# Sums written over gathered rows, and 41 held parts of the table instead of 40

## The chip, the cores and the metric

The kernel runs on one core of one Trainium2 chip. The metric is the device time of one execution in microseconds (us); lower is better. The engines are named as the profile names them: PE (matrix multiply; its weight loads are PEld), DVE (vector), ACT (scalar), POOL (GpSimd, here the issuer of gathers) and SP (SyncE, the issuer of most transfers; SPq and ACTq are the issuing queues of SP and ACT).

## The reference, cut to what matters

```python
e = emb[seq]                                   # 1024 users, 50 steps, 128 numbers
prefix = jnp.cumsum(e, axis=1)
uF = prefix / jnp.minimum(t + 1, lengths)      # per step and user
y = (uF - mean_over_users) * rsqrt(var + 1e-5) * gamma + beta
# 50 steps, one after the other:
v = v + (x - v) / 2; spike = (v >= 1); v = v - spike
scores = spikes.mean(over steps) @ emb.T       # 1024 x 100001, float32
```

Row 0 of the table counts as zero. The output has 409.6 MB, the table 51.2 MB.

## The kernel before, in words

**Two stages.** The first runs the 50 steps (`for t in range(T)`, line 384). The second multiplies the spike counts (eight blocks of 128 users, `counts[0..7]`) with the transposed table, evicts, scales and stores. PE works in a format of about half the float32 digits, so each part of the table is *split* into a high and a low half and multiplied twice (`product`, lines 198 to 207).

**A step.** `gather(t)` (line 245) lets POOL issue eight indirect transfers of 128 rows each into a tile `e`; the pool `gather` has two such tiles, which alternate. In five steps (`BY_SYNC`: 12, 22, 31, 40, 49) it issues seven, and SP fetches the last 128 rows one by one (`fetch_singles`, line 261). PE transposes the rows onto running sums in PSUM (`pre`, line 391). DVE scales the sums into a tile `uF` of a pool of its own (line 402) and takes the statistics (403, 414). ACT takes the square root (418) and turns `uF` into mean minus `uF`, in place (425). DVE works out the factor `a` (431 to 444), ACT forms the scaled x in `vt` out of `uF` (line 448), and DVE adds the decayed old state (451). The gathers of step t+2 stand in the program right behind the statistics of step t (line 404), so they need the tile `e` of step t, which is free when PE has read it. POOL has nothing else to do in the steps.

**Parts.** The table has 98 parts of 1024 rows (the last has 673). A part is loaded as a tile of 128 partitions by 1024 numbers (4 KB in each partition). 40 are *held*: loaded while the steps run, 14 of them at the start, two more into places of parts 0 and 1, which are split in the steps 42 and 44 (lines 470 to 482), and 24 (groups 2 to 5 of six parts) when SP has issued its last single rows (line 409). The other 58 are loaded in the second stage, three at a time, by ACT's queue (`fetch`, line 141), into row tiles whose parts have been split.

`pick` (line 130) loads one part in three in another way: its rows on partitions 0 to 119 by an indirect transfer from POOL, the other eight partitions by ACT or by a second indirect transfer, with small dummy transfers (`turn_by`) between them. `PICKED` lists these parts.

**Splitting.** `prepare` (line 189) lets PE transpose a part (line 177), ACT copy the high half (193) and DVE subtract it for the low half (194). A pair of places for the halves must be free (`free`). At first there are two pairs and `third` (the tile `aside`, which held parts 2 and 3). When all six parts of a row tile have been split, its space becomes three pairs (`places`, line 546): after part 9 and after part 15.

**Products.** `WIDTHS` cuts the 98 parts into column blocks: four of two parts, four of three, thirteen of six. Column block 0 consists of parts 0 and 1, and so on. In each, the eight user blocks n follow one another; a part's product goes to one of four PSUM tiles and is evicted by ACT or DVE in turn (lines 605 and 607) into an output tile, and SP stores the whole output tile (`store`, line 209). Output tiles take turns (`turns`): four of two parts in column blocks 0 to 3, three of three parts in blocks 4 to 7, three of six parts from 8 on, of which two are row tiles. A tile is written again when its store has ended. `ready` (line 572) is called behind user blocks 2 to 6 and behind each part of block 7 (in column block 0 from 4, from 8 on from 0); it splits the next part if a pair is free and the part belongs to this column block, the next one, or one of the `FURTHER` ones. All engines work in program order.

Of the kernel before, what the change touches and what calls it, by code (L numbers as in the profile page):

```python
# [30 lines left out]
TWICE = 2  # L31
ASIDE = 2
SHIFT = TWICE + ASIDE
FURTHER = {5: 1, 6: 2}

# [4 lines left out]
SPARED = 120  # L40
PICKED = range(42, 97, 3)
TURN = 17
# [6 lines left out]
def rec_kernel(  # L49
# [46 lines left out]
    def pair(i):  # L96
        free.append([embp.tile([P, HALF], F32R, tag=f"{x}{i}", name=f"{x}_{i}") for x in ("hi", "lo")])

    def size(q):
        return min(HALF, N - q * HALF)  # L100
# [4 lines left out]
    def group(g):  # L105
        at = g if g < AHEAD else AHEAD - 2 + g % 2
        r = rowp.tile([P, GROUP, HALF], F32, tag=f"rows{at}", name=f"rows_{g}")
        for k in range(GROUP):
            rows[g * GROUP + SHIFT + k if g else k + ASIDE * (k >= TWICE)] = r[:, k, :]
        return r  # L110
# [76 lines left out]


    def prepare(q, pt):
        turned(q, pt)  # L190
        split[q] = hi, lo = free.pop(0)
        vp, vh, vl = views(q, pt, hi, lo)
        nc.scalar.copy(vh, vp)  # L193
        nc.vector.tensor_tensor(vl, vp, vh.bitcast(F32), ALU.subtract)  # L194
# [18 lines left out]
    with ExitStack() as ph:  # L213
        once = ph.enter_context(tc.tile_pool(name="once", bufs=1))
        lp = ph.enter_context(tc.tile_pool(name="lif", bufs=1))
        sp = ph.enter_context(tc.tile_pool(name="stats", bufs=3))
        up = ph.enter_context(tc.tile_pool(name="uF", bufs=1))
        gp = ph.enter_context(tc.tile_pool(name="gather", bufs=2))
# [11 lines left out]
        nc.sync.dma_start(out=gb[:, 1:2], in_=beta.rearrange("(d o) -> d o", o=1))  # L230
        first = group(0)
        fetch(first, 0, 0, TWICE)
        spare = asidep.tile([P, ASIDE, HALF], F32, tag="aside", name="spare")
        for k in range(ASIDE):
            rows[TWICE + k] = spare[:, k, :]
        fetch(spare, 0, TWICE, ASIDE)
        fetch(first, TWICE, SHIFT, GROUP - TWICE)
        for g in range(1, EARLY):
            fetch(group(g), 0, g * GROUP + SHIFT, GROUP)
# [34 lines left out]
        make_identity(nc, ident)  # L274
        isz = up.tile([P, NB, P], F32, tag="uF", name="isz")
        rb = up.tile([P, NB, P], F32, tag="uF", name="rb")
        gather(0)
# [31 lines left out]
        for n in range(NB):  # L309
            nc.tensor.transpose(rps[:, n * P : (n + 1) * P], rb[:, n, :], ident)  # L310
        rlen = once.tile([P, B], F32, tag="rlen", name="rlen")
        nc.vector.tensor_copy(rlen, rps)
# [71 lines left out]
        for t in range(T):  # L384
            last = t == T - 1
            e = es.pop(t)
            uF = up.tile([P, B], F32, tag="uF", name=f"uF_{t}")
            bs = sp.tile([P, B // BANK, 6], F32, tag="bs", name=f"bs_{t}")
            for h, cs in enumerate(halves):
# [13 lines left out]
                nc.vector.bn_stats(bs[:, h, :], uF[:, cs])  # L403
            if t + 2 < T:
                gather(t + 2)
            if t in BY_SYNC[:-1]:
# [46 lines left out]
            if not last:  # L453
                vt = vp.tile([P, B], F32, tag=f"v{(t + 1) % 2}", name=f"v_{t}")
                x(vt, whole)
                if t:
                    spiked(count, whole, v)
# [40 lines left out]
        o0 = gp.tile([P, HALF], F32, tag="e", name="o_0_0")  # L498
        o1 = gp.tile([P, HALF], F32, tag="e", name="o_0_1")
        firsts = [(q, po, o, h, cs) for q, po, o in ((0, po0, o0), (1, po1, o1)) for h, cs in enumerate(halves)]  # L500
# [42 lines left out]
    to_fetch = held  # L543
    third = None

    def places(at):
        t = rowp.tile([P, GROUP, HALF], F32R, tag=f"rows{at}", name=f"pairs_{at}")
        free.extend((t[:, k, :], t[:, k + 1, :]) for k in range(0, GROUP, 2))

    for c, W in enumerate(WIDTHS):  # L550

        if c in (0, NARROW, MIDDLE):
            opening.close()
            if c == NARROW:
                assert third in free
                free.remove(third)
                beside.close()
            where = opening if c < MIDDLE else ctx
            op = where.enter_context(tc.tile_pool(name="o", bufs=1, reuse_waits="tile"))
            if c == 0:  # L560
                turns = [(op, f"o{k}", 2) for k in range(4)]
            elif c == NARROW:
                turns = [(op, f"o{k}", 3) for k in (2, 0, 1)]
            else:
                fourth = op.tile([P, 4, HALF], F32R, tag="pairs", name="pairs")
                free.extend((fourth[:, k, :], fourth[:, k + 1, :]) for k in (0, 2))
                turns = [(rowp, "rows2", 6), (op, "o", 6), (rowp, "rows3", 6)]
            blocks = 0
        q1 = q0 + W
        q2 = q1 + (WIDTHS[c + 1] if c + 1 < len(WIDTHS) else 0)  # L570

        def ready():
            nonlocal to_split, third
            if to_split < q2 + FURTHER.get(c, 0) and free:
                prepare(to_split, psum.tile([P, HALF], F32, tag="ps", name=f"pt_{to_split}"))
                to_split += 1

                if to_split == SHIFT:
                    t = asidep.tile([P, ASIDE, HALF], F32R, tag="aside", name="third")
                    third = (t[:, 0, :], t[:, 1, :])  # L580
                    free.append(third)
                if to_split in (GROUP + SHIFT, 2 * GROUP + SHIFT):
                    places(to_split // GROUP - 1)

# [65 lines left out]
```

## Time and profile before

| | before |
|---|---|
| median of 3 runs | 1556.75 us (1555.91 to 1557.61) |
| the profiled execution | 1554.93 us |
| its span on the core | 1552.9 us |
| PE, DVE, ACT, POOL busy in it | 1129.4, 950.0, 674.7, 431.1 us |
| HBM read, written | 77.69 MB, 409.60 MB |
| mean granted clock of PE | 0.961 |

The span is the time from the first to the last instruction of the core. The page gives busy time by engine, digits for 40 equal slices (tenths of a slice), the chain of work that ended last, and groups of instructions by source line. In a timeline row stand the start, the duration, the engine, the line, the operation, the tile written and the tiles read, and in brackets the idle time of the engine before it and what ended it; "issue" means that the profile shows nothing that was waited for. In a row of a table of stretches stand from and to, the length, the busy time of PE, PEld, DVE, ACT and POOL with the number of instructions, the granted clock of PE, the mean busy share of the 16 DMA engines and the GB/s that they moved.

### The profile page before, as it was taken

The page shows a single profiled execution, that of the slowest core. Times are in us where ns is not written, and L with a number is a line of the kernel's source. Part 1 is how long each engine was busy: PE and PEld are TensorE (multiplying, and loading weights), DVE is VectorE, ACT ScalarE, POOL GpSimd, SP SyncE. Part 2 cuts the span into 40 slices and gives each one's busy share as a digit, 9 for nine tenths or more (in the row PEclk, how much of TensorE's full clock was granted, in tenths as well). Part 3 has the DMA queues.
Part 4 walks back from the last instruction along what each step waited for, and adds up shares of the span by engine and source line. Part 5 has one row for each costly group of instructions (what it writes and reads, how often), then busy time and mean ns, then how long its engine had stood idle before and what let it go on. Part 6 is the DMA issues. An engine that isn't in the chain of part 4 may idle for free.

```text
span 1552.9 us, 13699 instructions
## 1 busy us (share of the span) xinstructions
PE 1129.4 (73%) x4465; PEld 799.3 (51%) x4465; DVE 950.0 (61%) x1128; ACT 674.7 (43%) x698; POOL 431.1 (28%) x462
## 2 busy tenths in 40 slices
PE   4444444454445998899988888887888888888894
PEld 2111111121222776677766666665666666666673
DVE  5777777677778656666555555554655555555552
ACT  3333333343334545555444444444444444444542
POOL 7777777777776000000010100101000010100000
PEclk9999999999999999999999998999989898999998
DMA  6222222832221999999999999999999999999999
GB/s 241 55 55 54 54 55 54 303 127 53 53 79 46 371 412 410 424 412 398 433 418 431 424 429 428 426 426 425 427 425 429 425 424 431 426 429 428 426 426 385
DMA packets 54315, 488.22 MB, mean 314 GB/s; under 512 B 12383, under 2 KB 13280, under 8 KB 33124
## 3 DMA queue, kind: packets, MB, share of 16 engines
q1 hardware_dynamic: 32176, 431.19, 66.0%
q0 software_dynamic: 16656, 35.60, 8.0%
q10 hardware_dynamic: 5412, 20.56, 3.2%
q8 instruction: 35, 0.57, 0.1%
q14 instruction: 36, 0.29, 0.1%
HBM read 77.69 MB, written 409.60 MB: 314 GB/s over the span
## 4 chain that ended last, share of the span: by engine, by line
DMA 42%; POOL 20%; PE 18%; issue 11%; DVE 5%; ACT 4%; ACTq 0%; SPq 0%; DVEq 0%; POOLq 0%
DMA scores<-o 40%; POOL e L248 20%; PE po L201 17%; DVE o L605 3%; ACT o L607 3%; DMA e<-in_L_rec_emb_table,idx 2%; DVE pairs L194 1%; ACT pairs L193 1%; PE pt L177 1%; ACT hi L193 0%; PE pre L391 0%; DVE lo L194 0%; PE warm L377 0%; DMA idx<-in_r_seq 0%; ACTq L607 0%
## 5 line engine op out<-in xcount | busy, mean ns | idle before, releaser
L605 DVE TENSOR_SCALAR o<-po 128x1024 f32<-128x1024 f32 (+1 forms) x390 | 467.6, 1215 | 307.6 <-PE po L201 154.3
L607 ACT ACTIVATE o<-po 128x1024 f32<-128x1024 f32 x392 | 393.4, 1025 | 487.7 <-DMA scores<-o 320.7
L248 POOL DMA_INDIRECT e<-in_L_rec_emb_table,idx x395 | 374.2, 947 | 122.4 <-issue 118.3
L391 PE MATMUL pre<-ident,e 128*128 128x128 f32 x395 | 174.7, 463 | 222.0 <-DMA e<-in_L_rec_emb_table,idx 221.7
L201 PE MATMUL po<-pairs,countB 128*128 128x512 f32 (+1 forms) x1120 | 287.8, 403 | 42.7 <-ACT o L607 42.7
L201 PE MATMUL po<-pairs,countC 128*128 128x512 f32 (+1 forms) x840 | 244.0, 438 | 61.2 <-ACT o L607 55.2
L201 PEld LDWEIGHTS po<-pairs,countB 128*128 128x128 f32 x1120 | 207.0, 189 | 104.4 <-ACT o L607 58.8
L391 PEld LDWEIGHTS pre<-ident,e 128*128 128x128 f32 x395 | 72.8, 185 | 327.0 <-DMA e<-in_L_rec_emb_table,idx 325.4
L201 PEld LDWEIGHTS po<-pairs,countC 128*128 128x128 f32 x840 | 170.1, 210 | 115.1 <-ACT o L607 65.4
L123 POOL DMA_INDIRECT rows<-in_L_rec_emb_table,picks x19 | 18.6, 980 | 636.3 <-PE pt L177 633.6
L194 DVE TENSOR_TENSOR pairs<-pt,pairs 128x1024 fp32r<-128x1024 f32 x70 | 85.3, 1218 | 101.5 <-ACT pairs L193 101.4
L402 DVE SCALAR_TENSOR_TENSOR uF<-rlen,pre 128x512 f32<-128x512 f32 x100 | 68.3, 683 | 101.9 <-PE pre L391 101.9
L177 PE MATMUL pt<-ident,rows 128*128 128x128 f32 (+1 forms) x768 | 106.0, 284 | 10.0 <-DVE rows L174 4.9
L177 PEld LDWEIGHTS pt<-ident,rows 128*128 128x128 f32 (+1 forms) x768 | 95.2, 148 | 27.2 <-issue 10.8
L418 ACT ACTIVATE r<-mv,eps 128x1 f32<-128x1 f32 x50 | 14.8, 295 | 213.8 <-DVE mv L414 213.8
L201 PE MATMUL po<-hi,countB 128*128 128x512 f32 x208 | 85.8, 412 | 12.5 <-ACT o L607 11.0
L349 PE MATMUL pre<-zT,ls 128*128 128x512 f32 x100 | 78.1, 783 | 22.5 <-DVE uF L402 18.5
L193 ACT CAST pairs<-pt 128x1024 fp32r<-128x1024 f32 x70 | 70.0, 1012 | 40.2 <-PE pt L177 40.2
L115 POOL DMA_INDIRECT turned_by<-in_L_rec_emb_table,picks x30 | 28.7, 956 | 209.8 <-DMA turned_by<-in_L_rec_emb_table,picks 198.7
L201 PE MATMUL po<-lo,countB 128*128 128x512 f32 x208 | 83.6, 402 | 0.0
L361 ACT ACTIVATE d<-v,less 128x1024 bf16<-128x1024 f32 x49 | 54.6, 1114 | 65.4 <-DVE v L451 62.3
L201 PE MATMUL po<-hi,countC 128*128 128x512 f32 x156 | 67.3, 432 | 13.8 <-ACT o L607 12.7
(99 smaller groups left out, 996.6 us busy)
## 6 DMA issues: line engine op xcount, KB each, us to landing
scores<-o SPq DMA_DIRECT2D x96, 3072.0 KB
scores<-o SPq DMA_DIRECT2D x32, 1536.0 KB
scores<-o SPq DMA_DIRECT2D x29, 1024.0 KB
scores<-o SPq DMA_DIRECT2D x8, 2896.5 KB
rows<-in_L_rec_emb_table ACTq DMA_DIRECT2D x19, 1024.0 KB
rows<-in_L_rec_emb_table SPq DMA_DIRECT2D x5, 3072.0 KB
held_rows<-in_L_rec_emb_table SPq DMA_DIRECT2D x640, 0.5 KB
e<-in_L_rec_emb_table,idx POOLq DMA_INDIRECT x395, 2.5
```

What stands on the lines that cost most here:

```text
L115: nc.gpsimd.indirect_dma_start(out=turned_by[:m, :], out_offset=None, in_=table.rearrange("n (k d) -> (n k) d", d=2), in_offset=bass.Indir ...
L177: nc.tensor.transpose(pt[:, k0 : k0 + pw], r[:pw, k0 : k0 + D], ident[:pw, :pw])
L193: nc.scalar.copy(vh, vp)
L194: nc.vector.tensor_tensor(vl, vp, vh.bitcast(F32), ALU.subtract)
L201: nc.tensor.matmul(po[:, :kw], lhsT=counts[n], rhs=part[:, k0 : k0 + kw], start=j == 0, stop=j == 1,)
L248: nc.gpsimd.indirect_dma_start(out=es[t][:, n * P : (n + 1) * P], out_offset=None, in_=table, in_offset=bass.IndirectOffsetOnAxis(ap=idx[: ...
L349: nc.tensor.matmul(pre[h], lhsT=l, rhs=zT[:, h * BANK : (h + 1) * BANK], start=t == 0, stop=False, skip_group_check=True,)
L361: nc.scalar.activation(d, v, AF.Identity, bias=less)
L391: nc.tensor.matmul(pre[h][:, k : k + P], lhsT=singles[t] if h * BANK + k + P == B and t in singles else e[:, h * BANK + k : h * BANK + k + P],
L402: nc.vector.scalar_tensor_tensor(uF[:, cs], rlen[:, cs], 1.0 / (t + 1), pre[h], ALU.max, ALU.mult)
L605: nc.vector.tensor_scalar_mul(o[:, h0 : h0 + hw], po[:, :hw], 1.0 / T)
L607: nc.scalar.mul(o[:, h0 : h0 + hw], po[:, :hw], 1.0 / T)
```

## The change

- The pool `uF` is gone: `uF = e`. DVE writes the scaled sums over the gathered rows of the step. `gather(t + 2)` moves down behind `x(vt, whole)`, so that it waits for line 448 of step t in place of the transposes.
- `isz` and `rb` of the preamble use the space of `negv`, and `rlen` becomes the second half of a new tile `shared`, whose first half holds part 4.
- 41 parts are held. Group 0 and 1 become six tiles of two parts (`two0` to `two10`), each loaded by a transfer of its own; `two0` is loaded twice, as before. The start loads 15 parts in eight transfers, where it were 14 in four.
- A tile of two parts becomes one pair of places when both have been split (`EMPTIED`: behind parts 6, 8, 10, 12, 14 and 16). `third` is free behind part 3 and is not used for parts from 8 on (`place_for`).
- In column blocks 0 and 1 there are three output tiles; from column block 2 on `shared` is the fourth.
- 57 parts are loaded in the second stage, 18 of them by `pick`, in 19 transfers of three; `FURTHER` lets column block 7 split one part more.
- One of the first outputs lies in `zT` in place of a gather tile.

```diff
-ASIDE = 2
+ASIDE = 3
 SHIFT = TWICE + ASIDE
-FURTHER = {5: 1, 6: 2}
+EMPTIED = {SHIFT + 2 + k: f"two{(k + 2) % GROUP if k < GROUP else k}" for k in range(0, 2 * GROUP, 2)}
+FURTHER = {5: 1, 6: 2, 7: 1}
...
-PICKED = range(42, 97, 3)
+PICKED = range(43, 95, 3)
...
+    def two(k, q):
+        r = rowp.tile([P, 2, HALF], F32, tag=f"two{k}", name=f"two_{q}")
+        rows[q], rows[q + 1] = r[:, 0, :], r[:, 1, :]
+        return r
...
+    def place_for(q):
+        return next((i for i, p in enumerate(free) if q < NARROW * WIDTHS[0] or p is not third), None)
...
-        split[q] = hi, lo = free.pop(0)
+        split[q] = hi, lo = free.pop(place_for(q))
...
-        up = ph.enter_context(tc.tile_pool(name="uF", bufs=1))
...
-        first = group(0)
+        first = two(0, 0)
         fetch(first, 0, 0, TWICE)
-        spare = asidep.tile([P, ASIDE, HALF], F32, tag="aside", name="spare")
-        for k in range(ASIDE):
+        spare = asidep.tile([P, ASIDE - 1, HALF], F32, tag="aside", name="spare")
+        shared = asidep.tile([P, 2, HALF], F32, tag="shared", name="shared")
+        for k in range(ASIDE - 1):
             rows[TWICE + k] = spare[:, k, :]
-        fetch(spare, 0, TWICE, ASIDE)
-        fetch(first, TWICE, SHIFT, GROUP - TWICE)
-        for g in range(1, EARLY):
+        rows[SHIFT - 1] = shared[:, 0, :]
+        rlen = shared[:, 1, :]
+        fetch(spare, 0, TWICE, ASIDE - 1)
+        fetch(shared, 0, SHIFT - 1, 1)
+        for k in range(2, 2 * GROUP, 2):
+            q = k + ASIDE + 2 * (k >= GROUP)
+            fetch(two(k, q), 0, q, 2)
+        for g in range(2, EARLY):
             fetch(group(g), 0, g * GROUP + SHIFT, GROUP)
...
-        isz = up.tile([P, NB, P], F32, tag="uF", name="isz")
-        rb = up.tile([P, NB, P], F32, tag="uF", name="rb")
+        isz = once.tile([P, NB, P], F32, tag="negv", name="isz")
+        rb = once.tile([P, NB, P], F32, tag="negv", name="rb")
...
-        rlen = once.tile([P, B], F32, tag="rlen", name="rlen")
...
-            uF = up.tile([P, B], F32, tag="uF", name=f"uF_{t}")
+            uF = e
...
-            if t + 2 < T:
-                gather(t + 2)
...
                 x(vt, whole)
+                if t + 2 < T:
+                    gather(t + 2)
...
-        o1 = gp.tile([P, HALF], F32, tag="e", name="o_0_1")
+        o1 = once.tile([P, HALF], F32, tag="zT", name="o_0_1")
...
-                turns = [(op, f"o{k}", 2) for k in range(4)]
+                turns = [(op, f"o{k}", 2) for k in range(3)]
...
+        elif c == 2:
+            assert to_split >= SHIFT
+            turns.append((asidep, "shared", 2))
...
-                if to_split == SHIFT:
-                    t = asidep.tile([P, ASIDE, HALF], F32R, tag="aside", name="third")
+                if to_split == SHIFT - 1:
+                    t = asidep.tile([P, ASIDE - 1, HALF], F32R, tag="aside", name="third")
                     third = (t[:, 0, :], t[:, 1, :])
                     free.append(third)
-                if to_split in (GROUP + SHIFT, 2 * GROUP + SHIFT):
-                    places(to_split // GROUP - 1)
+                if to_split in EMPTIED:
+                    t = rowp.tile([P, 2, HALF], F32R, tag=EMPTIED[to_split], name=f"pair_{to_split}")
+                    free.append((t[:, 0, :], t[:, 1, :]))
```

More of the change, by code (lines that the diff above doesn't have):

```diff
@@ L108, in group @@
         for k in range(GROUP):
-            rows[g * GROUP + SHIFT + k if g else k + ASIDE * (k >= TWICE)] = r[:, k, :]
+            rows[g * GROUP + SHIFT + k] = r[:, k, :]
         return r
@@ L185, in views @@
         )
+    third = None
+    def place_for(q):
+        return next((i for i, p in enumerate(free) if q < NARROW * WIDTHS[0] or p is not third), None)
     def prepare(q, pt):
         turned(q, pt)
-        split[q] = hi, lo = free.pop(0)
+        split[q] = hi, lo = free.pop(place_for(q))
         vp, vh, vl = views(q, pt, hi, lo)
@@ L543, in rec_kernel @@
     to_fetch = held
[L544 to L548, printed above, removed]
     for c, W in enumerate(WIDTHS):
@@ L554, in rec_kernel @@
             if c == NARROW:
-                assert third in free
-                free.remove(third)
+                assert any(p is third for p in free)
+                free[:] = [p for p in free if p is not third]
                 beside.close()
@@ L573, in ready @@
             nonlocal to_split, third
-            if to_split < q2 + FURTHER.get(c, 0) and free:
+            if to_split < q2 + FURTHER.get(c, 0) and place_for(to_split) is not None:
                 prepare(to_split, psum.tile([P, HALF], F32, tag="ps", name=f"pt_{to_split}"))
                 to_split += 1
-                if to_split == SHIFT:
-                    t = asidep.tile([P, ASIDE, HALF], F32R, tag="aside", name="third")
+                if to_split == SHIFT - 1:
+                    t = asidep.tile([P, ASIDE - 1, HALF], F32R, tag="aside", name="third")
                     third = (t[:, 0, :], t[:, 1, :])
                     free.append(third)
-                if to_split in (GROUP + SHIFT, 2 * GROUP + SHIFT):
-                    places(to_split // GROUP - 1)
+                if to_split in EMPTIED:
+                    t = rowp.tile([P, 2, HALF], F32R, tag=EMPTIED[to_split], name=f"pair_{to_split}")
+                    free.append((t[:, 0, :], t[:, 1, :]))
         blockwise = [(n, q) for n in range(1 if c == 0 else 0, NB) for q in range(q0, q1)]
```

## The prediction

> **What bounds the kernel now.** I read the page first, its slices above all, for they show two kernels in one.
>
> ```profile
> span 1552.9 us, 13699 instructions
> ...
> DMA  6222222832221999999999999999999999999999
> ...
> DMA 42%; POOL 20%; PE 18%; issue 11%; DVE 5%; ACT 4%; ACTq 0%; SPq 0%; DVEq 0%; POOLq 0%
> ```
>
> For the first third the DMA engines are mostly idle, apart from a load at the start and a burst in slices 8 and 9; these are the 50 steps. Then the DMA digits are all 9: the products, whose stores and loads fill the DMA engines. The chain agrees: POOL (GpSimd) and issue hold 31% of the span, DMA 42%. To see what kind of bound each is, I took the groups of lines (busy and mean ns, then idle time and what ended it) and the table of stretches (the last two columns are the DMA share and GB/s).
>
> ```profile
> L248 POOL DMA_INDIRECT e<-in_L_rec_emb_table,idx x395 | 374.2, 947 | 122.4 <-issue 118.3 <-DMA idx<-in_r_seq 2.3 <-PE pre L391 1.2
> 280.00:330.00 50.00, 23.45 (x51) 9.77 (x51) 35.56 (x61) 18.17 (x20) 37.80 (x41) 1.00 0.83 304
> 900.00:1000.00 100.00, 81.24 (x359) 63.13 (x358) 53.23 (x46) 44.07 (x45) 8.47 (x9) 0.94 1.01 427
> ```
>
> All 395 gathers go back to back: of 122.4 us idle, 118.3 is "issue" (0.30 each), and the 1.2 us put down to PE are four times that same 0.30. GpSimd never waits for a tile. So the steps last as long as GpSimd needs for its list of gathers, and **a microsecond that GpSimd is made to wait is never won back**. In the products the DMA share is 1.01 at 427 GB/s: there a byte less is time won, and a moment in which no store is queued is time lost.
>
> **The change, part by part.** The profiled run took 1554.93 us (span 1552.9); the median of the runs shown is 1556.75, 1.82 above it. I sum against 1554.93 and add 1.82 at the end. What a measurement of this kernel can tell from no change is about 0.2%, 3.1 us.
>
> *The step's tile is held longer.* Before, a gather tile is free once PE has transposed it; after, when ACT has read the scaled sums out of it (line 448), since they now lie in it. The gathers of step t+2 need that tile, so the question is whether line 448 of step t ends before GpSimd reaches them. Steps have eight gathers, five of them seven, so each can be counted off. The timeline gives start and duration.
>
> ```profile
> 3.33 0.19 DVE L280 CAST ids<-idx 128x50 f32<-128x50 int32 x1 [3.33 <-DMA idx<-in_r_seq]
> 3.59 1.14 POOL L248 DMA_INDIRECT e<-in_L_rec_emb_table,idx  x1 [2.27 <-DMA idx<-in_r_seq]
> 3.56 0.47 SPq L148 DMA_DIRECT2D spare<-in_L_rec_emb_table  x1
> ...
> 23.90 1.21 ACT L448 ACTIVATE v<-uF,hgb,a 128x1024 f32<-128x1024 f32 x1
> 24.64 0.94 POOL L248 DMA_INDIRECT e<-in_L_rec_emb_table,idx  x1 [0.30 <-PE pre L391]
> ...
> 208.66 1.21 ACT L448 ACTIVATE v<-uF,hgb,a 128x1024 f32<-128x1024 f32 x1 [0.64 <-DVE a L444]
> 213.15 0.94 POOL L248 DMA_INDIRECT e<-in_L_rec_emb_table,idx  x1 [0.31 <-issue]
> ...
> 301.19 1.21 ACT L448 ACTIVATE v<-uF,hgb,a 128x1024 f32<-128x1024 f32 x1 [0.64 <-DVE a L444]
> 301.81 0.94 POOL L248 DMA_INDIRECT e<-in_L_rec_emb_table,idx  x1 [0.30 <-PE pre L391]
> ...
> 320.31 1.21 ACT L448 ACTIVATE v<-uF,hgb,a 128x1024 f32<-128x1024 f32 x1 [0.63 <-DVE a L444]
> 320.53 0.94 POOL L248 DMA_INDIRECT e<-in_L_rec_emb_table,idx  x1 [0.30 <-PE pre L391]
> ```
>
> The first pair gives the price of a wait: the same transfer released DVE at 3.33 and GpSimd's gather at 3.59, so a gather starts about 0.3 us after its release. An ordinary step (19, with the gathers of 21) ends line 448 at 208.66 + 1.21 = 209.87, and the gathers start at 213.15: 3.28 us in hand, 3.0 after the 0.3. No cost there. Three steps have nothing in hand. Step 0 starts late and ends at 25.11, when gather 24.64 has gone out: a wait of 0.47 + 0.3 = 0.77. In the burst of 280 to 330 (304 GB/s: the loads of the groups 2 to 5) the gathered rows land later and the step ends later. Step 28 ends at 302.40 against 301.81: 0.59 + 0.3 = 0.89. Step 30 ends at 321.52 against 320.53: 0.99 + 0.3 = 1.29. Every wait moves the later gathers and their steps alike, so the waits add: **+2.95**. Behind the waiting gather stand only more gathers, and PE and DVE of that step wait for those. The lower bound is 0.77, if the burst falls so that the other two vanish (SyncE issues four more loads at the start, at 0.47 each by the row of `spare`, and so reaches it 1.9 us later); the upper is 3.5, for the start carries one part more and can make step 1 late too. I take the sum: GpSimd and burst shift by about the same amount.
>
> *One part less is loaded in the products.* 1024 x 512 bytes, 0.524 MB, at 427 GB/s: **-1.23**. Its load goes to the start instead. Bounds -1.23 and 0 (first rival).
>
> *Places for split parts come free two by two.* Before, the third pair and a group's three pairs were all there was, so part 7 was split at the last chance, part 9 with part 10 too. Following `ready` through both versions, part 7 is now split at block 3 of its predecessor, part 9 likewise, and only part 10 is left for the end of column block 3. Three dips of the DMA rate belong to these ends (the row of 706 is for a later part):
>
> ```profile
> 566.00:568.00 2.00, 2.00 (x6) 1.53 (x5) 1.59 (x2) 0.00 (x0) 0.00 (x0) 0.50 0.80 332
> 586.00:588.00 2.00, 1.66 (x5) 0.86 (x5) 2.00 (x2) 0.04 (x1) 0.00 (x0) 1.00 0.70 291
> 590.00:592.00 2.00, 2.00 (x10) 1.59 (x9) 1.23 (x1) 1.11 (x2) 0.00 (x0) 1.00 0.71 297
> 706.00:708.00 2.00, 2.00 (x10) 1.63 (x9) 2.00 (x3) 1.03 (x1) 0.00 (x0) 1.00 0.79 330
> ```
>
> Against 427 the first loses 2 x (1 - 332/427) = 0.44 us, the second 0.64, the third 0.61. The first and third go; the second stays, for a split still stands there: **-1.05**, bounds 0 and -1.69.
>
> *Three output tiles instead of four in column blocks 0 and 1.* The fourth is the tile with part 4, and comes in column block 2. What it costs shows best at the end of column block 1:
>
> ```profile
> 506.40 1.36 SPq L210 DMA_DIRECT2D scores<-o  x3
> 506.00:508.00 2.00, 1.77 (x7) 0.86 (x6) 1.89 (x4) 1.95 (x4) 0.00 (x0) 1.00 0.37 137
> ...
> 540.74 1.03 ACT L607 ACTIVATE o<-po 128x1024 f32<-128x1024 f32 x1 [1.60 <-DMA scores<-o]
> 542.70 1.23 DVE L194 TENSOR_TENSOR lo<-pt,hi 128x1024 fp32r<-128x1024 f32 x1 [3.35 <-ACT hi L193]
> 543.84 2.37 DVE L605 TENSOR_SCALAR o<-po 128x1024 f32<-128x1024 f32 x2
> 545.12 1.48 SPq L210 DMA_DIRECT2D scores<-o  x2
> ...
> 556.84 1.03 ACT L607 ACTIVATE o<-po 128x1024 f32<-128x1024 f32 x1 [1.56 <-DMA scores<-o]
> ...
> 562.05 1.03 ACT L607 ACTIVATE o<-po 128x1024 f32<-128x1024 f32 x1 [1.58 <-DMA scores<-o]
> ```
>
> Stores free a tile every 2.60 us (556.84 to 562.05 is two of them). Block 7 got its tile at 540.74; a split's cast and its subtraction (542.70) come behind it, and its store goes out at 545.12. With three tiles it waits for one store more: 543.34, and the store goes out at 547.7. At 540.74 three stores were still under way, which last to 540.74 + 3 x 2.60 = 548.5 as counted by the freeing of tiles. Bytes trail an issue by about a microsecond: the first stores are issued at 506.40, and 506 to 508 has 0.37 of its 2 us in use, so they start at 507.3. I estimate the same for a freeing behind the last byte. So the engines run out at 547.5 and start again at 548.7: 1.2 us. An ordinary block takes 1.2 us from tile to store, and with two stores of 2.60 queued nothing runs dry. **+1.2**, bounds 0 (the trailing times are shorter) and 3.0 (the same again where column block 0 opens and ends).
>
> *One more split at the end of column block 7* (the new entry of `FURTHER`), one less in block 8. There DVE is behind already:
>
> ```profile
> 705.52 1.22 DVE L194 TENSOR_TENSOR pairs<-pt,pairs 128x1024 fp32r<-128x1024 f32 x1
> 706.65 2.35 DVE L605 TENSOR_SCALAR o<-po 128x1024 f32<-128x1024 f32 x2
> ```
>
> The subtraction of 1.22 at 705.52 holds back the last eviction, and the DMA dip of 706 to 708 (0.79) is there. A second one puts another 1.2 in front of that store; the split that block 8 is spared gives part of it back, in dips that are as short. **+0.7**, bounds 0 and 1.2.
>
> *The rest at nothing:* `rlen` in half a tile, `isz` and `rb` under `negv`, the last load of three parts, the second first output in `zT`. All are ahead of or beside the waits above; uncovered, they cost a fraction of a step, inside the 3.5.
>
> Sum: 2.95 - 1.23 - 1.05 + 1.2 + 0.7 = +2.57; 1554.93 + 2.57 + 1.82 = **1559.3**.
>
> **The rivals.**
>
> *The DMA engine of the last eight partitions sets the pace.* `pick` spares the rows from 120 on in some loads: before in 19 of 58 loaded parts, after in 18 of 57, which leaves 39 unspared both times. If the engine that serves these rows bounds the products, the part less wins nothing: +3.80, 1560.6. Against it: a mean share of 1.01 over 16 engines leaves none of them idle to wait for a slower one. The profile shows no single engine, so it is not excluded. The Trainium skill (DMA: Bandwidth & Descriptors, section Latency and other measured facts) says that DMA engines 7 and 15 are usually slower than the others in traces; no run here shows it, and by that rule this rival would hold.
>
> *GpSimd's waits in the burst vanish.* If the burst starts 1.9 us later and GpSimd only 0.77, the steps 28 and 30 may end in time: 0.77 in place of 2.95, +0.39, 1557.1. With the bounds of the dips as well, a gain reaches -2.2. For it: the shortfalls, 0.59 and 0.99, are smaller than that shift. Against it: the burst lasts through four steps, and some step lies at its end wherever it starts.
>
> *Slower: three tiles starve the stores.* It decides when tile-to-store takes more than the 5.2 us of two queued stores less the two trailing microseconds, 3.2. Evictions in pairs take 1.2; with a split between, the rows above show 545.12 - 540.74 = 4.4. If PE, too, stands still while four PSUM tiles wait, ordinary blocks lose about 0.4 each: 12 x 0.4 = 4.8 in place of 1.2, +6.17, 1562.9. Against it: at column block 4 three tiles already serve, with bigger stores.
>
> **How the numbers follow.** My case 0.50, the vanished waits 0.25, the slow engine 0.13, the starved stores 0.12. My case reaches past +3.1 in three of ten, since its middle is at +2.57 and its terms are uncertain by about 1; the vanished waits stay within, and 0.06 of it is kept for a gain over 3.1, which lies outside every bound above; the slow engine is half and half. Slower: 0.15 + 0.12 + 0.07 = 0.34; faster 0.06; the same 0.60. The range takes in the vanished waits with the best dips (1556.75 - 2.2 = 1554.6) and the starved stores: 1554.6 to 1563.0.
>
> **What would show it.** Right: L248 shows idle time put down to ACT L448, about 3 us in three places (near 25, 302 and 322), and the last gather comes that much later; the dips at 566 and 590 are gone, new ones stand near 548 and 708; loads issued by ACT carry one part less. Wrong: waits of GpSimd in ordinary steps (then the tile is held longer than line 448, and every step would pay), no waits at all, or a DMA rate below 427 in the long middle.

## The result and the profile after

| | before | after |
|---|---|---|
| median (16 runs each, one chip) | 1556.26 us (1554.94 to 1558.40) | 1560.11 us (1559.12 to 1561.12) |
| ratio, 95% interval | | 1.0025 (1.0018 to 1.0032) |
| profiled execution, its span | 1554.93, 1552.9 us | 1560.22, 1558.4 us |
| first store issued | 506.40 us | 509.27 us |
| first store to the end of the span | 1046.5 us | 1049.1 us |

The change costs 3.85 us, 0.25%. The forecast was 1559.3 us, +2.57. The last two rows say where it went: 2.87 us into the steps, 2.6 us into the products. That makes 5.5 for two single executions, which overstates it: before's profiled one lay 1.3 below its median. In the experiments, three executions on one chip were in a slower state, at 2020, 1942 and 1672 us, and are left out of the medians.

The page of the changed kernel looks like the page of before; the chain has moved its shares from POOL and issue to DMA, though the steps are as long as ever. So it is no measure of what bounds them.

```profile
span 1558.4 us, 14089 instructions
...
DMA  7222222832121899999999999999999999999998
...
DMA 50%; PE 19%; POOL 13%; issue 6%; DVE 6%; ACT 4%; ACTq 0%; SPq 0%; DVEq 0%; POOLq 0%
```

The waits of the changed kernel up to the end of the steps (total, times, longest) have a line that before did not have, and the timeline has the places.

```profile
POOL e L264 <- issue: 106.4, 349, 0.3
...
POOL e L264 <- ACT v L461: 4.0, 4, 1.5
```

```profile
25.45 0.94 POOL L264 DMA_INDIRECT e<-in_L_rec_emb_table,idx  x1 [1.17 <-ACT v L461]
...
291.85 1.21 ACT L461 ACTIVATE v<-e,hgb,a 128x1024 f32<-128x1024 f32 x1 [0.50 <-DVE a L457]
293.33 0.94 POOL L264 DMA_INDIRECT e<-in_L_rec_emb_table,idx  x1 [1.00 <-ACT v L461]
...
323.24 0.94 POOL L264 DMA_INDIRECT e<-in_L_rec_emb_table,idx  x1 [1.52 <-ACT v L461]
...
499.71 0.94 POOL L264 DMA_INDIRECT e<-in_L_rec_emb_table,idx  x1 [0.30 <-issue]
```

Of four waits for line 461 one is the usual 0.30; the others exceed it by 0.87, 0.70 and 1.22. The pair at 291.85 shows the mechanism: line 461 ends at 293.06 and the gather starts 0.27 later. The last gather stands at 499.71, in before at 496.97: 2.74 later. Nothing between the three places was made up or lost.

The long middle runs as before: over the 700 us from 300 us behind the first store, both kernels move 427 GB/s. The part less is one of GpSimd's: the whole traffic of its queue falls from 35.60 to 35.07 MB, while ACT's stays at 20.56. The prediction's sign, a part less in the loads that ACT issues, was wrong in this.

For the products, both profiles are cut at the same distances behind their first store: 0 to 10 us, 20 to 25, 35 to 45, 60 to 100, 100 to 300. The last column is GB/s. Before, then after:

```profile
506.40:516.40 10.00, 8.45 (x36) 6.38 (x35) 6.57 (x9) 5.73 (x7) 0.00 (x0) 1.00 0.79 308
526.40:531.40 5.00, 5.00 (x28) 4.13 (x27) 3.30 (x3) 2.88 (x4) 0.00 (x0) 1.00 1.01 419
541.40:551.40 10.00, 8.24 (x33) 6.21 (x32) 5.88 (x5) 4.62 (x6) 0.00 (x0) 0.83 1.01 415
566.40:606.40 40.00, 38.05 (x176) 30.00 (x176) 25.53 (x22) 21.16 (x21) 0.00 (x0) 0.97 0.97 402
606.40:806.40 200.00, 182.46 (x843) 141.78 (x841) 124.74 (x105) 103.27 (x104) 3.58 (x4) 0.99 0.99 418
```

```profile
509.27:519.27 10.00, 8.46 (x36) 6.35 (x35) 6.39 (x8) 4.61 (x6) 0.00 (x0) 1.00 0.67 258
529.27:534.27 5.00, 4.96 (x21) 3.65 (x20) 2.29 (x2) 3.71 (x4) 0.00 (x0) 1.00 0.79 323
544.27:554.27 10.00, 7.17 (x32) 5.24 (x33) 4.88 (x5) 4.37 (x5) 0.00 (x0) 1.00 0.84 346
569.27:609.27 40.00, 35.93 (x169) 26.99 (x168) 23.81 (x20) 21.55 (x22) 0.00 (x0) 1.00 1.01 416
609.27:809.27 200.00, 182.88 (x839) 141.83 (x838) 125.18 (x106) 103.47 (x105) 2.75 (x3) 0.99 0.99 415
```

Each row loses length x (1 - rate / 427), against the 427 GB/s of the long middle. Before: 2.79, 0.09, 0.28, 2.34 and 4.22 us. After: 3.96, 1.22, 1.90, 1.03 and 5.62. So +1.17 where column block 0 opens, +1.13 at its end, +1.62 at the end of column block 1, -1.31 at the ends of blocks 2 and 3, and +1.40 in the 200 us behind that. With -1.23 for the bytes of the part not loaded this is +2.78, against 2.6 by the spans. The three dips that the prediction named look so in the changed kernel, at the same distances behind the first store:

```profile
568.87:570.87 2.00, 2.00 (x10) 1.63 (x9) 0.98 (x1) 1.00 (x1) 0.00 (x0) 1.00 1.04 430
588.87:590.87 2.00, 1.62 (x8) 0.93 (x6) 0.00 (x0) 1.93 (x2) 0.00 (x0) 1.00 1.03 426
592.87:594.87 2.00, 2.00 (x10) 1.37 (x9) 1.84 (x3) 1.03 (x1) 0.00 (x0) 1.00 0.88 365
```

The first is gone, as forecast. The second, forecast to stay, is gone too, and the third, forecast to go, keeps 0.29 of 0.61 us.

The timeline of the changed kernel shows the opening gap and the one at the end of column block 1:

```profile
513.54 1.96 ACT L621 ACTIVATE o<-po 128x1024 f32<-128x1024 f32 x2 [2.59 <-PE po L212]
513.56 1.22 DVE L619 TENSOR_SCALAR o<-po 128x1024 f32<-128x1024 f32 x1 [1.42 <-PE po L212]
...
548.56 1.02 ACT L621 ACTIVATE o<-po 128x1024 f32<-128x1024 f32 x1 [1.72 <-DMA scores<-o]
549.48 1.01 ACT L204 CAST hi<-pt 128x1024 fp32r<-128x1024 f32 x1
550.37 1.04 ACT L621 ACTIVATE o<-po 128x1024 f32<-128x1024 f32 x1
550.52 1.23 DVE L205 TENSOR_TENSOR lo<-pt,hi 128x1024 fp32r<-128x1024 f32 x1 [3.46 <-ACT hi L204]
551.66 2.37 DVE L619 TENSOR_SCALAR o<-po 128x1024 f32<-128x1024 f32 x2
```

The first eviction of column block 0 starts 4.27 us behind the first store, in before 1.73 (508.13). ACT and DVE start together there, as if one thing had released both. At 548.56 block 7 gets its tile, and cast and subtraction come ahead of the second eviction that its store needs, as forecast.

### The profile page after: what moved, and what is told of

Read it like the earlier page. It is cut to its first block, busy times and chain, and to the rows that moved or that the text cites. A ratio compares the mean times of both kernels' runs of the same rounds, so it can differ in the third digit from the quotient of the medians.

```text
span 1558.4 us, 14089 instructions
## 1 busy us (share of the span) xinstructions
PE 1132.6 (73%) x4465; PEld 796.1 (51%) x4465; DVE 948.7 (61%) x1128; ACT 678.9 (44%) x698; POOL 427.4 (27%) x458
## 3 DMA queue, kind: packets, MB, share of 16 engines
q0 software_dynamic: 16416, 35.07, 7.7%
q10 hardware_dynamic: 5412, 20.56, 3.2%
## 4 chain that ended last, share of the span: by engine, by line
DMA 50%; PE 19%; POOL 13%; issue 6%; DVE 6%; ACT 4%; ACTq 0%; SPq 0%; DVEq 0%; POOLq 0%
DMA scores<-o 42%; PE po L212 14%; POOL e L264 13%; DMA e<-in_L_rec_emb_table,idx 8%; DVE o L619 3%; ACT o L621 3%; PE pre L406 2%; PE pre L364 2%; DVE e L417 1%; DVE pair L205 1%; PE pt L183 1%; ACT pair L204 0%; DVE lo L205 0%; ACT hi L204 0%; PE warm L392 0%
## 5 line engine op out<-in xcount | busy, mean ns | idle before, releaser
L212 PE MATMUL po<-pair,countB 128*128 128x512 f32 x912 | 241.6, 404 | 29.2 <-ACT o L621 29.0
L212 PE MATMUL po<-pair,countC 128*128 128x512 f32 (+1 forms) x684 | 198.1, 430 | 31.9 <-ACT o L621 26.5
L212 PEld LDWEIGHTS po<-pair,countB 128*128 128x128 f32 x912 | 169.8, 190 | 79.8 <-ACT o L621 41.7
L212 PEld LDWEIGHTS po<-pair,countC 128*128 128x128 f32 x684 | 135.4, 205 | 75.0 <-ACT o L621 34.6
L417 DVE SCALAR_TENSOR_TENSOR e<-shared,pre 128x512 f32<-128x512 f32 x100 | 68.3, 683 | 104.2 <-PE pre L406 104.2
L205 DVE TENSOR_TENSOR pair<-pt,pair 128x1024 fp32r<-128x1024 f32 (+1 forms) x57 | 69.2, 1215 | 63.6 <-ACT pair L204 63.6
L183 PE MATMUL pt<-ident,rows 128*128 128x128 f32 x648 | 87.6, 280 | 0.7 <-ACT o L621 0.6
L183 PEld LDWEIGHTS pt<-ident,rows 128*128 128x128 f32 x648 | 79.1, 146 | 14.4 <-issue 1.4
L418 DVE BATCH_NORM_STATS2 bs<-e 128x6 f32<-128x512 f32 x100 | 69.4, 694 | 3.5
```

The lines of the kernel that those rows point to most:

```text
L183: nc.tensor.transpose(pt[:, k0 : k0 + pw], r[:pw, k0 : k0 + D], ident[:pw, :pw])
L212: nc.tensor.matmul(po[:, :kw], lhsT=counts[n], rhs=part[:, k0 : k0 + kw], start=j == 0, stop=j == 1,)
L417: nc.vector.scalar_tensor_tensor(uF[:, cs], rlen[:, cs], 1.0 / (t + 1), pre[h], ALU.max, ALU.mult)
```

## The experiments

The experiments ran on four chips. On three of them the kernel before itself took 1714.15, 1718.66 and 1724.03 us, on the fourth, that of the last two kernels, 1556.48. The kernel before was not profiled on the first three. In their other profiles the steps are longer, and so are the products where the group loads come late; where these loads are done before the products, the products are as long everywhere. So each ratio is against the kernel before on the same chip, and the products are read from the profiles.

**hold_only**: the kernel before with the hold alone. One of the first outputs lies in the space of `uF`, which the hold empties.

```
-            uF = up.tile([P, B], F32, tag="uF", name=f"uF_{t}")
+            uF = e
...
-            if t + 2 < T:
-                gather(t + 2)
...
                 x(vt, whole)
+                if t + 2 < T:
+                    gather(t + 2)
```

> The kernel before with the hold alone: the scaled sums are written over the gathered rows and the gathers of step t+2 come behind line 448, but 40 parts are held, with the row tiles, the four output tiles and the products of before. Theory of the sum: GpSimd waits three times for ACT (about 0.87, 0.7 and 1.2 us, at steps 0, 27 and 30), so the last gather and the first store come 2.75 us later and nothing later changes: +2.8 us. Rival (the waits of GpSimd are made up for in the products, which are bound by the DMA engines anyway): waits in the trace, but the time within 0.5 us of the kernel before.

Measured: 1724.48 us, ratio 1.0071 (1.0043 to 1.0098): +10.3 us, well over both expectations. The rival falls; my size does not hold on this chip either. GpSimd waits 16 times for ACT:

```profile
POOL e L248 <- ACT v L446: 138.0, 16, 13.1
```

What these chips do without the hold shows in the next kernel.

**three_only**: the kernel before with three output tiles in column blocks 0 and 1.

```
-                turns = [(op, f"o{k}", 2) for k in range(4)]
+                turns = [(op, f"o{k}", 2) for k in range(3)]
...
+        elif c == 2:
+            turns.append((op, "o3", 2))
```

> The kernel before with three output tiles in place of four in the column blocks 0 and 1, the fourth from block 2 on; nothing else. Theory of the sum: two gaps of the DMA engines, of 1.1 and 1.6 us, about 21 and 43 us behind the first store, and no gap at the opening: +2.7 us. Rival (the gaps of the changed kernel are those of the opening, whose first output tile lies over a tile that a store still reads, and run on from there): both gaps small here, under 0.5 us each.

Measured: 1716.97 us, 1.0017 (0.9993 to 1.0042), which tells nothing. Its waits within the steps do:

```profile
DVE uF L402 <- remote: 113.9, 20, 10.0
...
POOL e L248 <- PE pre L391: 58.7, 8, 17.2
POOL e L248 <- remote: 49.0, 16, 4.7
```

DVE's scaling stands still 20 times for up to 10 us, released by something that the profile does not name ("remote"), and GpSimd then runs out of tiles, without a hold too. Its waits for PE and for that come to 112 us in all; in hold_only it waits 138 us for ACT, and the first store comes at 663.1 in place of 647.8. SyncE's single rows are slow too: 619 us for 640, against 269 in the changed kernel on the first chip. So the group loads come last and run into the first column blocks, where they fill what three tiles leave empty. Only one split falls behind them: its subtraction starts at 699.92, and 701 to 703 moves 143 GB/s, a loss of 2 x (1 - 143/427) = 1.33 us, near the 1.6 expected at the end of column block 1. The gap comes without the changed opening, so there the rival is wrong. At the end of column block 0 the group loads hide whatever gap there is.

**twos_only**: the kernel before with row tiles of two parts, loaded and used as in the changed kernel, and so places for splits two by two.

```
-                if to_split in (GROUP + SHIFT, 2 * GROUP + SHIFT):
-                    places(to_split // GROUP - 1)
+                if to_split in EMPTIED:
+                    t = rowp.tile([P, 2, HALF], F32R, tag=EMPTIED[to_split], name=f"pair_{to_split}")
+                    free.append((t[:, 0, :], t[:, 1, :]))
```

> The kernel before with the row tiles of two parts and their earlier places alone; 40 parts held, a tile of their own for the sums, four output tiles. Theory of the sum: the dips of the DMA rate 60 to 100 us behind the first store go, and the rest stays: -1.5 us. Rival (these dips went in the changed kernel because the DMA engines were late by then and had more queued): the dips stay and the time is that of before within 0.5 us.

Measured: 1711.80 us, 0.9995 (0.9967 to 1.0022), unclear. By rates, the 40 us from 60 us behind the first store ran at 416 GB/s in place of hold_only's 406 (hold_only first):

```profile
723.10:763.10 40.00, 34.54 (x156) 25.83 (x155) 23.11 (x20) 19.82 (x20) 0.00 (x0) 1.00 0.98 406
707.70:747.70 40.00, 36.52 (x171) 27.80 (x169) 24.02 (x20) 19.88 (x20) 0.00 (x0) 1.00 1.01 416
```

That is 1.03 us lost, not 1.97: -0.94, between rival and theory and near the term of -1.05. Late group loads lie in the products of both kernels, more of them in twos_only, whose products are 7 us longer; three_tiles_twos, below, is the cleaner test.

**no_picks**: the changed kernel, all parts loaded as whole tiles.

```
-        wide = whole - (whole == n and q + whole - 1 in PICKED)
+        wide = whole
```

> The changed kernel, in which no part is loaded in the other way (no indirect transfer, no spared rows; the dummy transfer ahead of the products stays). Theory of the sum (no single DMA engine sets the pace, a part less is worth its bytes): within 2 us of the changed kernel. Rival (the engine of the last eight partitions sets the pace, so that the part less won nothing): 18 parts put 18 x 32 KB more on that engine, at a sixteenth of 427 GB/s up to 22 us more.

Measured: 1741.14 us (one run), 1074.9 from the first store on; the changed kernel itself was not run on this chip. In 400 us of the middle, no_picks and then the kernel after on its own chip:

```profile
1200.00:1600.00 400.00, 335.57 (x1432) 260.90 (x1431) 212.54 (x178) 176.33 (x178) 0.00 (x0) 0.93 1.00 420
```

```profile
1100.00:1500.00 400.00, 339.86 (x1471) 263.89 (x1470) 220.17 (x186) 182.28 (x184) 22.85 (x24) 0.94 1.01 426
```

Without the 18 picked loads the rate falls, and the share still reads 1.00. So something in whole loads does set a pace, and my theory is wrong for a kernel without picks. The Trainium skill (DMA: Bandwidth & Descriptors, section Latency and other measured facts) says that engines 7 and 15 are usually slower, by its best guess through the transfers that GpSimd issues. The lower rate would fit a slower engine, but no run shows which, and the rate fell when GpSimd issued fewer transfers, so this case does not bear that cause out.

Whether the pace binds with the picks in place stays open. That the rate is then that of before decides nothing, since the rival leaves 39 unspared parts in both kernels and so foresees equal rates. The size speaks against it: over the 700 us from 300 us behind the first store no_picks runs at 422 GB/s, which loses 8.2 us against 427. Over its whole products it runs at 415, where spread, below, runs at 419: 30.2 us lost, not 19.8. Were that engine the bound with the picks too, the loss would be up to 22 us more, by the estimate of the expectation. But the reason that I gave against the rival, a mean share of 1.01, is worth nothing: the share cannot tell 420 GB/s from 426.

**hold_only_2** is hold_only again, **spread** the changed kernel with its four group loads apart.

```
-                if t == BY_SYNC[-2]:
-                    for g in range(EARLY, AHEAD):
-                        fetch(group(g), 0, g * GROUP + SHIFT, GROUP)
+                g = EARLY + BY_SYNC.index(t)
+                fetch(group(g), 0, g * GROUP + SHIFT, GROUP)
```

> The kernel before with the sums written over the gathered rows and the next gathers behind x, 40 parts held and nothing else changed, a second time. My theory: three waits of GpSimd for line ACT v, about 0.8, 0.7 and 1.2 us, none in ordinary steps, and the whole of it stays in the time: 2.8 us over the kernel before (ratio 1.0018, bounds 1.0010 to 1.0025). Rival, that the hold is hidden and the loss of the change comes from the products: at most 0.5 us over (ratio up to 1.0003). On the chip of the run before, whose steps stall for other reasons, it cost 10.3 us, and more waits: if steps stall here too, that is expected again.

> The changed kernel with the loads of groups 2 to 5 issued one each at the steps 12, 22, 31 and 40, in place of all four at step 40's single rows. My theory: the waits of GpSimd near 293 and 323 us come from the burst alone, so both go (0.7 + 1.2 = 1.9 us), the first, near 25 us, stays; against the kernel before, +3.85 - 1.9 = +2.0 us (ratio 1.0013). Rival: each load of 3 MB makes a burst of its own, as long as 7 us, and some step lies in it; then waits of 0.5 to 1 us come in up to four places and the time is that of the changed kernel or up to 1 us more (ratio 1.0025 to 1.0031).

Measured, on another chip whose steps stall: 1736.12 us, 1.0110 (1.0078 to 1.0142), and 1734.72, 1.0096 (1.0062 to 1.0131). In both, GpSimd waits for ACT some 150 us (15 times, up to 22 and 18 us). The hold alone costs as much there as the changed kernel with its loads apart. Whether spreading wins 1.9 us cannot be read among such stalls.

**n_before, n_after, n_hold, n_all**: four kernels without SyncE's single rows, in the hope of quiet steps. The edit common to all:

```
-BY_SYNC = (12, 22, 31, 40, 49)
+BY_SYNC = ()
+LOADED = (26, 26, 26, 26)
...
+            if t in LOADED:
+                nc.sync.load([seen[LOADED.index(t)]], mv[0:1, 0:1].bitcast(I32))
+            for k, at in enumerate(LOADED):
+                if t == at:
+                    fetch(group(EARLY + k), 0, (EARLY + k) * GROUP + SHIFT, GROUP)
```

n_hold has the hold besides, with a first output in the space of `uF` as in hold_only. n_all has besides `LOADED = (8, 18, 28, 38)`, `count` and `ls` placed first in their pool, and in column blocks 0 and 1 `turns = [(op, f"o{k}", 1) for k in range(6)]` with a store for each part; the tiles of the later blocks lie in a pool opened anew at block 2.

> The kernel before without SyncE's single rows: all 50 steps have eight gathers, and the loads of groups 2 to 5 start when the statistics of step 26 are there, near 280 us as before. Theory: the slow steps of the last runs (stalls of gathers up to 10 us, SyncE's rows at half their rate) come of SyncE's single rows and GpSimd's gathers getting in each other's way, so the stalls go, first store near 512 us in place of 650 to 675: 1556.3 + 5 x 1.25 = 1562.5 us. Rival: the gathers stall by themselves on these chips, and the time stays above 1690.

> The changed kernel, altered the same way. Theory: as far from its base as the two were without this, +3.85 us over n_before (2 to 5): waits of GpSimd for ACT v at the second step and in the burst, 2.7 us together, and 2.4 us of gaps in the stores of column blocks 0 and 1, less 1.2 for the part that is not loaded. Rival, that the difference came with the five steps of seven gathers and their rows: within 1 us of n_before.

> Only the hold of the step's tile, on n_before. Theory: the waits of GpSimd for ACT v come in the second step and in the burst, none elsewhere, and n_before + 2.7 us (1.5 to 3.5), the first store as much later, the products unchanged. Rival, that most of the change's loss comes from the products: at most +0.5.

> n_after with three mends: the group loads one by one at the steps 8, 18, 28 and 38 in place of a burst; the count and ls tiles placed so that the first output tile of column block 0 does not lie over zT, out of which a first output is still being stored; six output tiles of one part, each stored by itself, in column blocks 0 and 1 in place of three of two parts. Theory: the waits in the burst go (-1.9 us), the gap where column block 0 opens goes (-1.2), and those at the ends of column blocks 0 and 1 go for the most part (-2): n_after - 5, which is n_before - 1.2 (0 to -2.5). Rival: the gaps only move (more stores, more waits), and n_all stays above n_before by 1 us or more.

Measured: n_before 1630.03 us, n_hold 1653.88, n_after 1655.64, n_all 1659.73, where the kernel before took 1724.03 (ratios 0.9474, 0.9611, 0.9609 and 0.9636, each with an interval of 0.004 to 0.0055 on either side). Without the single rows the time is 94 us shorter, and the steps still stall. Both my theory and its rival on these stalls are half right; their cause stays open. The waits of GpSimd in n_before and in n_hold:

```profile
POOL e L249 <- remote: 41.3, 9, 5.7
POOL e L249 <- PE pre L336: 24.5, 6, 5.7
```

```profile
POOL e L249 <- ACT v L434: 80.2, 13, 9.0
```

n_hold costs 23.9 us over n_before by the medians. In the two profiled executions it is 14.2, as much as GpSimd's waits grow, from 66 to 80 us. n_after, 1.8 above n_hold, cannot be told from it by time. The products are 1046.6 us long in n_before, 1047.0 in n_hold, 1049.2 in n_after and 1048.7 in n_all: the same 2.6 us between n_before and n_after as between the original pair, on another chip and with other steps. The hold does not touch the products. The five stretches of n_before, n_after and n_all:

```profile
580.32:590.32 10.00, 8.35 (x35) 6.50 (x34) 5.42 (x7) 5.22 (x7) 0.00 (x0) 0.96 0.74 286
600.32:605.32 5.00, 5.00 (x27) 4.18 (x26) 3.54 (x3) 2.88 (x4) 0.00 (x0) 1.00 1.01 418
615.32:625.32 10.00, 7.94 (x38) 6.02 (x37) 5.95 (x5) 5.35 (x6) 0.00 (x0) 1.00 0.99 404
640.32:680.32 40.00, 37.86 (x168) 29.76 (x168) 25.21 (x22) 20.26 (x21) 0.00 (x0) 0.93 0.96 397
680.32:880.32 200.00, 181.96 (x849) 141.98 (x848) 125.05 (x106) 103.92 (x105) 3.09 (x4) 1.00 1.00 419
```

```profile
613.70:623.70 10.00, 8.48 (x36) 6.39 (x35) 6.37 (x8) 4.60 (x6) 0.00 (x0) 1.00 0.67 258
633.70:638.70 5.00, 4.96 (x21) 3.65 (x20) 2.25 (x2) 3.73 (x4) 0.00 (x0) 1.00 0.78 321
648.70:658.70 10.00, 7.51 (x29) 5.41 (x30) 5.00 (x5) 3.88 (x4) 0.00 (x0) 0.88 0.87 358
673.70:713.70 40.00, 36.92 (x174) 27.93 (x174) 24.67 (x21) 21.55 (x22) 0.00 (x0) 1.00 1.01 417
713.70:913.70 200.00, 181.40 (x838) 140.56 (x837) 125.03 (x105) 103.27 (x105) 2.76 (x3) 1.00 0.99 415
```

```profile
609.30:619.30 10.00, 9.14 (x35) 6.84 (x34) 5.40 (x7) 5.16 (x7) 0.00 (x0) 0.83 0.73 281
629.30:634.30 5.00, 5.00 (x25) 3.83 (x24) 3.21 (x3) 2.37 (x3) 0.00 (x0) 1.00 1.03 406
644.30:654.30 10.00, 7.83 (x28) 5.39 (x28) 5.18 (x5) 4.25 (x5) 0.00 (x0) 0.83 0.98 382
669.30:709.30 40.00, 35.96 (x171) 27.17 (x170) 23.91 (x20) 21.67 (x22) 0.00 (x0) 1.00 1.00 413
709.30:909.30 200.00, 182.22 (x837) 141.41 (x836) 125.17 (x105) 103.02 (x105) 2.75 (x3) 0.99 0.98 414
```

n_after against n_before: +0.66, +1.13, +1.08, -1.87 and +1.87 us, and -1.23, together 1.6 of the 2.6; the rest lies outside these stretches. The gaps of the first three rows are in the changed kernel both times. n_all fills them in part: 3.42, 0.25 and 1.05 us where n_after loses 3.96, 1.24 and 1.62. But its stores of one part run at 406 GB/s with a full share, where n_before's stores of two ran at 418 in the same 5 us, and it gives most of that back: 0.5 us shorter, not the 3 expected. The rival, that the gaps only move, was right about it. That its time is yet above n_after's lies in its steps, whose stalls vary (1646 to 1666 us).

**n_three_tiles**: n_hold with the space of `uF`, which the hold empties, as a third gather tile. **three_tiles_twos**: the kernel before with this, and the places two by two.

```
-        up = ph.enter_context(tc.tile_pool(name="uF", bufs=1))
-        gp = ph.enter_context(tc.tile_pool(name="gather", bufs=2))
+        gp = ph.enter_context(tc.tile_pool(name="gather", bufs=3))
```

> n_hold with the space of uF, which it leaves empty, given to a third gather tile. Theory: the hold costs because it takes away what GpSimd has in hand before it needs the tile again: about 7 us before, 3.3 us held, 13 us with three tiles. Then stalls of gathers of up to 10 us no longer reach GpSimd, nor do the waits at step 2 and in the burst: its idle time falls to the 0.3 us of each gather (120 us in all; 186 in n_before, 201 in n_hold), the first store comes near 515 us and the time is about 1566 us (1560 to 1580) on any chip. Rival: each late landing stops PE and DVE by itself, however early GpSimd is; then the time stays near n_before's, 1610 to 1640 where gathers stall.

> The kernel before with the sums written over the gathered rows, a third gather tile in the space of uF, places for split parts two by two, 40 parts held and four output tiles: the parts of the change that gain, without those that cost. Theory: on a chip whose gathers do not stall, 1.0 to 1.4 us faster than before, from the dips at the ends of column blocks 2 and 3, with no wait of GpSimd. Where they stall, SyncE's single rows (627 us for 640 of them, where it took 270) set the end of the steps, so the third tile can win little there: 0 to 2% faster than before. Rival: the third tile helps as much as without single rows, 5% or more.

Measured, on the chip without stalls: n_three_tiles 1560.80 us, 1.0036 (1.0023 to 1.0049); three_tiles_twos 1555.46, 0.9995 (0.9987 to 1.0004). The waits of GpSimd for ACT in the steps of the one and of the other:

```profile
POOL e L248 <- ACT v L433: 0.3, 1, 0.3
```

```profile
POOL e L260 <- ACT v L458: 0.6, 2, 0.3
```

Nothing but the usual 0.30 is left, with the sums still written over the gathered rows and the burst of loads still there. The +4.3 us of n_three_tiles are less than its five gathers more, 6.2 us at 1.25 each; in the profiles its first store comes 5.5 us later than that of before, and the products are as long, 1046.5 us. What gives the rest back was not traced. three_tiles_twos is 1.0 us under before, as expected and less than can be told apart. Its products are 1045.8 us long, and the 40 us from 60 behind the first store lose 1.78 us in place of 2.34:

```profile
567.40:607.40 40.00, 35.46 (x168) 27.83 (x167) 24.23 (x21) 21.60 (x22) 0.00 (x0) 0.96 0.99 408
```

Whether a third tile helps where steps stall was not seen, since this chip's do not: the rival to that stays open.

## Why the prediction was right, and where not

**The hold, +2.95: right, 2.74.** It is three waits and none in ordinary steps. One fell a step earlier than named, at 293.33 in place of 302: the burst began 1.3 us later, and the step at its front paid, 0.70 for 0.89. The rival of vanished waits is wrong. That the hold on two tiles is the cause is shown from two sides where steps are quiet: the kernel with it waits for line 461 where before does not, and with a third tile the waits are gone. The middle place was named a step off, so that its size came near is in part luck. What I took for a constant is none: "no cost there", 3 us in hand in an ordinary step, holds for quiet steps only. Where steps end up to 10 us late, the hold cost 10, 17 and 24 us, four to nine times as much.

**The part less, -1.23: not shown.** The bytes are saved: the stretches' losses against 427 GB/s, with this term, give the length of the products to 0.2 and 1.0 us. But a pace set by one slow engine would put a loss of the same size back somewhere, and of the 1.4 and 1.9 us that the last stretch loses more, most is unexplained and has room for it. no_picks speaks against this rival by its size only, and my own reason against it was worth nothing. It stays open.

**Places two by two, -1.05: near in size, wrong in place.** The stretch gains 0.6 us in three_tiles_twos, 0.9 in twos_only, 1.3 in the changed kernel and 1.9 in n_after. The sum counted the first and the third dip as gone and the second as staying; the second went, and the third kept half. That the errors cancel is luck.

**Three output tiles, +1.2: the step that failed in size.** The sum held one gap, at the end of column block 1, and left "the same again where column block 0 opens and ends" to the bound of 3.0. All three are there, in both pairs: 3.9 and 2.9 us. The end of block 1 is shown by three_only (1.33). The end of block 0 meets the same condition, a split between tile and store, and should have been in the sum; no run isolates it. At the opening, n_all moved the first output away from under the tile and won 0.5 of 0.7 to 1.2; it changed the stores too, so the cause there is only made likely. The rival of starved stores, with ordinary blocks losing too, is wrong: the 20 us between these places (10 to 20 and 25 to 35 behind the first store) lose 0.4 us in both kernels.

**One more split, +0.7: sized well where it lies.** The 8 us around the dip at the end of column block 7 (704 to 712 in before) lose 1.99 in place of 1.22, in the second pair 1.82 in place of 1.03; over the 20 us from 200 behind the first store 0.3 and 0.6 remain, since the stretch behind gives some back. The whole 200 us lose 1.4 and 1.9 us more, over the bound of 1.2. The rest is spread over the stretch and its cause is open; the slow engine's 1.23 us could be in it.

So the total came out near, +3.85 for +2.57, with the largest term right to 0.2 us, and with the output tiles under-counted by about 2 us. Its nearness is partly luck: the terms as the profiled pair shows them come to the 5.5 of that pair, of which 1.3 is the low execution of before. The absolute figure is nearer still, 1559.3 for 1560.11, since the three runs of before that it started from lay 0.5 above the median of the sixteen.

## What to carry to other kernels

Before a buffer is held longer, work out how much time its producer has in hand in every kind of step, the first one and those under a burst of loads too: each shortfall is paid in full when the producer is the bound. Space that such a merging of buffers frees may be worth more as another buffer of the same kind than as one more piece of held data. And where one end of a stretch shows a gap, every end that meets the same condition belongs in the sum.

## What the runs showed of the hardware

- The same kernel took 1556 us here and 1714 to 1724 on three chips of the experiments. The long middle of the products runs at 427 GB/s on all of them. Most of the 160 us or so lies in the steps: in three_only the first store comes 141 us later than in before, and the products are 13.5 us longer, with late loads in them. DVE's scaling waits there up to 10 us, 20 times in 50 steps, without a releaser in the profile, and 640 single-row transfers take SyncE 619 us in place of 269. Without the single rows, 94 of those us go.
- The mean DMA share reads 1.00 to 1.03 at 427 GB/s, at 420, and at 406 with small stores. Only the GB/s show the loss.
- The granted clock of PE lay between 0.81 and 0.97 in single runs of the changed kernel, and their times within 0.13%.
